# Output normalised on ScalarE and scaled on VectorE in whole-tile instructions, reciprocals on GpSimd: a cross-attention kernel on one core

## The chip, the cores and the metric

The kernel runs on one core of one Trainium2 chip. Times are device microseconds of one execution, and the time of a kernel is the median of its runs. The engines are named as in the profile: PE (TensorE) with PEld for its weight loads, DVE (VectorE), ACT (ScalarE), POOL (GpSimd) and SP, which here only issues DMAs.

## What is computed

For 64 batches, x is 256x512 and the context c is 256x384, all in float32:

```python
text_p  = x @ W_text + b_text            # 256x512
audio_p = c @ W_audio + b_audio          # 256x512
Q = layer_norm(text_p, g1, beta1)
K = layer_norm(audio_p, g2, beta2)
alpha = softmax(Q @ K.T / sqrt(512))
H = (alpha @ audio_p) @ W_out + b_out
out = layer_norm(H + x, g_out, beta_out)
```

`layer_norm` takes mean and variance over the last axis of 512, with 1e-5 added to the variance.

## The kernel before, in words

The batches go through a software pipeline written out by hand (`manual_schedule`): every engine runs its instructions in the order in which the code issues them. A batch's 256 rows are two tiles of 128 partitions, and most tensors are [128, 2, 512] or its transpose in four chunks.

One pass of the loop `for b in range(B - 2)` (L856) works on several batches at once:

- `at = Attention(b)`: scores of batch b into PSUM (`ps_sc`, L511), the negated row maxima on DVE (`maxima`, L521, tile `nmx`), the exponentials on ACT with their row sums in `den` (`exponentials`, L528), the reciprocals of the sums on DVE (`reciprocals`, L538, `rden`), the division of the exponentials on ACT (`divide_e`, L542), their store to DRAM and fetch in squares of 32 rows, from which DVE's 32x32 transposes make the transposed tile in the next pass (`turn_e`).
- q and then k of batch b + 2 (`Blocks`, L454 to L497): a product of 256 rows by 512 columns is made of seven half-size products in the manner of Strassen. `products` (L465) gives PE one or two of them for one PSUM bank; the pool `p_pj` has six banks, taken in turn. `leave` (L476, the adds of L483) evicts one product on DVE and adds it into the rows. The sums of inputs that the seven products need are formed by POOL (`sum_x`, L304 to L307, tile `xsum`; `sum_c`, L319 to L322, tile `csum`, or `zsum` for the output).
- After q and k, ACT squares the rows to get the variance (`square`, L380), POOL makes the reciprocal root by an add and a power of -0.5 (`rstd_of`, L335 to L344), ACT scales the rows (`normalise`, L408), SP stores them (`store`, L418). They are fetched in squares a pass later (`fetch`), transposed on DVE (`turn`, L91 and L439), and scaled and shifted per column on ACT (`affine`, L446, tiles `qT` and `kT`).
- `turn_next(b + 3)` (L728) transposes the inputs of batch b + 3 on DVE and forms their sums on POOL: `turn_x`, `sum_x`, `turn_c`, `sum_c`.
- `last` is the batch one pass older, b - 1: its context (`context`, L577), copied to `zT` by ACT (L584), the sums of that (`start_products`) and the seven output products (tile `ps_y`, rows `yr`), of which three are evicted at the head of the next pass.
- `done` is the batch two passes older, b - 2: after those evictions POOL adds x (`add_x`, L593), ACT takes sum and squares (`statistics`, L601 and L606, the negated mean `nm` and the sum of squares `ssq`), and DVE finishes the rows with two instructions for each of the two tiles: `shift` (L694), (y + nm) * g_out, and `settle` (L703), y * r + beta_out. SP stores the output (`store`, L713).

Head (batches 0 and 1) and tail (after the loop) are written out separately; in the tail `shift` and `settle` are used as well.

The order of one pass around the change is, as the code has it: scores, the last three evictions and add_x of `done`, `turn_e`, `turn_next`, maxima, exponentials, first q products and eviction, reciprocals, division, fetches and loads on SP, statistics of `done`, the other q products and evictions, squares of q, `q[b+1].turn`, the two shifts, context of `last`, affine of q, turn and affine of k, the two settles and the store of `done`, normalise and store of q, sums of zT, the whole of k, and then the output products of `last`.

Of the kernel before, what the change touches and what calls it, by code (L numbers as in the profile page):

```python
# [9 lines left out]
F32 = mybir.dt.float32  # L10
AF = mybir.ActivationFunctionType
ALU = mybir.AluOpType
# [3 lines left out]
P = 128  # L16
# [6 lines left out]
def kernel(  # L23
# [41 lines left out]
    nc = tc.nc  # L65
# [3 lines left out]
    H = w_text.shape[1]  # L69
    LT, ST = L // P, S // P  # L70
    DC, AC, HC = D // P, DA // P, H // P
    scale = 1.0 / math.sqrt(H)

    const = ctx.enter_context(tc.tile_pool(name="const", bufs=1))
# [4 lines left out]
    small = ctx.enter_context(tc.tile_pool(name="small", bufs=4))  # L79
# [26 lines left out]
    def load_squares(b):  # L106
        load_c(b)
        load_x(b)
# [23 lines left out]
    def row(v, name):  # L132
        t = const.tile([P, H], F32, tag=name, name=name)
        nc.sync.dma_start(t, v.rearrange("(o h) -> o h", o=1).broadcast_to([P, H]))
        return t
# [162 lines left out]
    def sum_x(xT):  # L298

        n = DC // 2  # L300
        part = lambda i, j: xT[:, j * n : (j + 1) * n, bass.ts(i, P)]
        s = work.tile([P, 4, n, P], F32, tag="xsum", name="xsum")
        add = nc.gpsimd.tensor_tensor
        add(s[:, 0], part(1, 0), part(1, 1), ALU.add)  # L304
        add(s[:, 1], s[:, 0], part(0, 0), ALU.subtract)  # L305
        add(s[:, 2], part(0, 0), part(1, 0), ALU.subtract)
        add(s[:, 3], part(0, 1), s[:, 1], ALU.subtract)  # L307
        ss = {
            1: part(0, 0), 2: part(0, 1), 4: part(1, 1),
            5: s[:, 0], 6: s[:, 1], 7: s[:, 2], 3: s[:, 3],  # L310
        }
        return {p: [ap[:, k, :] for k in range(n)] for p, ap in ss.items()}

    def sum_c(cT, tag="csum"):

        part = lambda i, j: cT[:, j, bass.ts(i, P)]
        s = work.tile([P, 5, P], F32, tag=tag, name=tag)
        add = nc.gpsimd.tensor_tensor
        add(s[:, 0], part(1, 0), part(1, 1), ALU.add)  # L319
        add(s[:, 1], s[:, 0], part(0, 0), ALU.subtract)  # L320
        add(s[:, 2:4], cT[:, 0:3:2, :P], cT[:, 0:3:2, P:], ALU.subtract)
        add(s[:, 4], part(0, 1), s[:, 1], ALU.subtract)  # L322
        return {
            1: [part(0, 0)], 2: [part(0, 1), part(0, 2)], 4: [part(1, 1), part(1, 2)],
            5: [s[:, 0], part(1, 2)], 6: [s[:, 1]], 7: [s[:, 2]], 3: [s[:, 4], s[:, 3]],
        }

    def weights_of_three(w_sb, name):
# [3 lines left out]
            ws[n].append(w_sb[:, 2, k2 * H2 : (k2 + 1) * H2])  # L332
        return ws

    def rstd_of(var, n, total=False):  # L335

        ve = small.tile([P, n], F32, tag="ve", name="ve")
        if total:
            nc.gpsimd.tensor_scalar(ve, var, 1.0 / D, EPS, ALU.mult, ALU.add)
        else:  # L340
            nc.gpsimd.tensor_scalar(ve, var, EPS, None, ALU.add)  # L341
        r = small.tile([P, n], F32, tag="rstd", name="rstd")
        nc.gpsimd.tensor_tensor(r, ve, nhalf[:, :n], ALU.pow)  # L343
        return [r[:, t : t + 1] for t in range(n)]  # L344

    class Projection:
# [57 lines left out]
        def normalise(self):  # L404
            for t in range(self.nt):
                row = self.rows[:, t, :]
                if self.centred:
                    nc.scalar.mul(row, row, self.r[t])  # L408
                else:
                    nc.scalar.activation(  # L410
                        row, row, AF.Identity, bias=self.nmr[:, t : t + 1], scale=self.r[t]
                    )
# [86 lines left out]
    class Attention:  # L499
# [36 lines left out]
        def reciprocals(self):  # L536
            self.rden = small.tile([P, LT], F32, tag="rden", name="rden")
            nc.vector.reciprocal(self.rden, self.den)  # L538

        def divide_e(self):  # L540
            for t in range(LT):
                nc.scalar.mul(self.e[:, t, :], self.e[:, t, :], self.rden[:, t : t + 1])  # L542
# [52 lines left out]
        def statistics(self):  # L595

            self.nm = small.tile([P, LT], F32, tag="nm", name="nm")
            self.ssq = small.tile([P, LT], F32, tag="ssq", name="ssq")
            for t in range(LT):
                junk = work.tile([P, D], F32, tag="junk", name="junk")  # L600
                nc.scalar.activation(  # L601
                    junk, self.y[:, t, :], AF.Identity, scale=-1.0 / D, accum_out=self.nm[:, t : t + 1]
                )
            for t in range(LT):
                junk = work.tile([P, D], F32, tag="junk", name="junk")
                nc.scalar.activation(  # L606
                    junk,
                    self.y[:, t, :],
                    AF.Square,
                    bias=self.nm[:, t : t + 1],  # L610
                    accum_out=self.ssq[:, t : t + 1],
                )
            self.r = dict(enumerate(rstd_of(self.ssq, LT, total=True)))

        def start_output(self):
            self.y = work.tile([P, LT, H], F32, tag="yr", name=f"y_{self.b}")
            self.mv = small.tile([P, LT, 2], F32, tag="mvy", name="mvy")
            self.ps_y = {}
# [99 lines left out]
    def turn_x(b):  # L718
        xT = work.tile([P, DC, L], F32, tag="xT", name=f"xT_{b}")
        turn(xT, blocks[b][1], DC)  # L720
        return xT

    def turn_c(b):
        cT = work.tile([P, AC, S], F32, tag="cT", name=f"cT_{b}")
        turn(cT, blocks[b][0], AC)
        return cT

    def turn_next(b):  # L728
        xT[b] = turn_x(b)
        xs[b] = sum_x(xT.pop(b))  # L730
        cT[b] = turn_c(b)
        cs[b] = sum_c(cT.pop(b))

    def add_bias(b):
        xb = rows[b][0]
# [4 lines left out]
    q, k, xT, cT, rows = {}, {}, {}, {}, {0: (x_0, c_0)}  # L740
# [31 lines left out]
    cs = {1: sum_c(cT[1])}  # L772
# [79 lines left out]
    go_sb = row(g_out, "go")  # L852
    beo_sb = row(beta_out, "beo")

    done = last = None
    for b in range(B - 2):  # L856
        three = b + 3 < B
        at = Attention(b)
        at.scores()
        if done:  # L860
            done.o.leave(3)
            done.o.leave(7)
            done.o.leave(4)
            done.add_x()
        if last:
            last.turn_e()
        if three and b:
            turn_next(b + 3)
        at.maxima()
        at.exponentials()  # L870
        q2 = q[b + 2] = Blocks("q", b + 2, xs.pop(b + 2), wt_blocks, bt_sb)
        q2.products(1, 2)
        q2.leave(1)
        at.reciprocals()
        at.divide_e()
        if b:
            q[b + 1].fetch()
            k[b + 1].fetch()
        at.store_e()
        if b + 4 < B:  # L880
            load_squares(b + 4)
        at.fetch_e()
        rows[b + 1] = load_rows(b + 1)
        if done:
            done.statistics()
        q2.products(6, 5)
        q2.leave(6)
        q2.leave(2)
        q2.leave(5)
        q2.products(7, 3)  # L890
        q2.leave(3)
        q2.leave(7)
        q2.products(4)
        q2.leave(4)
        q2.square()
        q2.scales()
        if three and not b:
            turn_next(b + 3)
        q[b + 1].turn()
        if done:  # L900
            done.shift(0)
            done.shift(1)
        if last:
            last.context()
        q[b + 1].affine(g1_sb, be1_sb)
        k[b + 1].turn()
        k[b + 1].affine(g2_sb, be2_sb)
        if done:
            done.settle(0)
            done.settle(1)  # L910
            done.store()
        q2.normalise()
        q2.store()
        if last:
            last.start_products()
        k2 = k[b + 2] = Blocks("k", b + 2, cs.pop(b + 2), wa_blocks, ba_sb)
        k2.products(1, 2)
        k2.leave(1)
        k2.products(6, 5)
        k2.leave(6)  # L920
        k2.leave(2)
        k2.leave(5)
        k2.products(7, 3)
        k2.leave(3)
        k2.leave(7)
        k2.products(4)
        k2.leave(4)
        k2.square()
        k2.scales()
        k2.normalise()  # L930
        k2.store()
        if last:
            last.o.products(1, 2)
            last.o.leave(1)
            last.o.products(6, 5)
            last.o.leave(6)
            last.o.leave(2)
            last.o.leave(5)
            last.o.products(7, 3)
            last.o.products(4)  # L940
        done, last = last, at


    at = Attention(B - 2)
# [112 lines left out]
```

## Time and profile before

| what | value |
|---|---|
| median of 3 runs | 1422.26 us (1420.84 to 1422.74) |
| the profiled execution | 1420.47 us, of which the span is 1418.70 us |
| mean granted TensorE clock | 0.998 |
| DMA | 322.61 MB, 227 GB/s over the span |
| ACT waits for nmx before the exponentials | 245.7 us in 64 waits |
| DVE waits for the exponentials before rden | 29.4 us in 60 waits |
| DVE waits for ps_q | 25.4 us in 107 waits |
| shift in the loop (L694) | 120 instructions, 726 ns each |
| settle (L703) | 124 instructions, 1065 ns each |

A row of the timeline gives the start in us from the start of the span, the duration from the first start to the last end of a group, the engine, the line, the operation, the tiles written and read, and the count; in brackets the idle time ahead of it and what ended it. A group of several instructions of one kind is one row, and consecutive instructions of an engine overlap by some tens of ns. Line numbers are those of the kernel before.

### The profile page before, as it was taken

The page shows a single profiled execution, that of the slowest core. Times are in us where ns is not written, and L with a number is a line of the kernel's source. Part 1 is how long each engine was busy: PE and PEld are TensorE (multiplying, and loading weights), DVE is VectorE, ACT ScalarE, POOL GpSimd, SP SyncE. Part 2 cuts the span into 40 slices and gives each one's busy share as a digit, 9 for nine tenths or more (in the row PEclk, how much of TensorE's full clock was granted, in tenths as well). Part 3 has the DMA queues.
Part 4 walks back from the last instruction along what each step waited for, and adds up shares of the span by engine and source line. Part 5 has one row for each costly group of instructions (what it writes and reads, how often), then busy time and mean ns, then how long its engine had stood idle before and what let it go on. Part 6 is the DMA issues. An engine that isn't in the chain of part 4 may idle for free.

```text
span 1418.7 us, 23330 instructions
## 1 busy us (share of the span) xinstructions
PE 1405.0 (99%) x6441; PEld 1220.9 (86%) x6441; DVE 1273.3 (90%) x2134; ACT 931.8 (66%) x2293; POOL 875.2 (62%) x1295
## 2 busy tenths in 40 slices
PE   9999999999999999999999999999999999999997
PEld 5788888888888888888888888888888888888885
DVE  5889999999999999999999999999999999999987
ACT  4666676676676676766766766766767667667662
POOL 5557556666666666566566665666665755666645
PEclk9999999999999999999999999999999999999999
DMA  8898887887888788788878887887887888788763
GB/s 207 228 246 229 242 244 209 242 240 216 237 233 234 228 230 238 233 226 236 244 217 236 239 224 228 238 229 229 229 238 232 225 239 242 216 238 241 205 200 109
DMA packets 450582, 322.61 MB, mean 227 GB/s; under 512 B 154900, under 2 KB 382996, under 8 KB 450452
## 3 DMA queue, kind: packets, MB, share of 16 engines
q1 hardware_dynamic: 450356, 320.98, 80.4%
q8 instruction: 53, 0.87, 0.3%
q14 instruction: 77, 0.63, 0.2%
q10 hardware_dynamic: 96, 0.13, 0.0%
HBM read 204.09 MB, written 116.92 MB: 226 GB/s over the span
## 4 chain that ended last, share of the span: by engine, by line
PE 94%; DMA 2%; DVE 1%; POOL 1%; SPq 1%; issue 1%; ACT 0%; POOLq 0%; DVEq 0%; ACTq 0%
PE ps_q L472 26%; PE ps_y L472 21%; PE ps_k L472 20%; PE ps_sc L511 15%; PE ps_z L577 11%; DMA qq<-qd 0%; DMA xq<-in_x_dram 0%; DMA qd<-qr 0%; DMA wt<-in_L_xattn_W_text_dram 0%; SPq L150 0%; DMA bt<-in_L_xattn_b_text_dram 0%; POOL rstd L343 0%; POOL ve L341 0%; DVE qr L483 0%; DVE st L267 0%
## 5 line engine op out<-in xcount | busy, mean ns | idle before, releaser
L341 POOL TENSOR_SCALAR ve<-var 128x2 f32<-128x2 f32 x126 | 43.6, 346 | 310.8 <-ACT junk L380 310.8
L511 PE MATMUL ps_sc<-kT,qT 128*128 128x256 f32 x1024 | 231.7, 379 | 1.9 <-ACT kT L446 1.9
L528 ACT ACTIVATE e<-ps_sc,nmx 128x256 f32<-128x256 f32 x128 | 59.5, 469 | 245.7 <-DVE nmx L521 245.7
L483 DVE TENSOR_TENSOR qr<-ps_q,qr 128x512 f32<-128x512 f32 x378 | 188.1, 511 | 35.8 <-PE ps_q L472 23.3
L511 PEld LDWEIGHTS ps_sc<-kT,qT 128*128 128x128 f32 x1024 | 194.2, 190 | 29.6 <-ACT kT L446 2.9
L483 DVE TENSOR_TENSOR kr<-ps_k,kr 128x512 f32<-128x512 f32 x378 | 188.2, 512 | 24.7 <-PE ps_y L472 0.5
L483 DVE TENSOR_TENSOR yr<-ps_y,yr 128x512 f32<-128x512 f32 x372 | 185.1, 511 | 24.1 <-DVE yr L483 0.9
L593 POOL TENSOR_TENSOR yr<-yr,x 128x512 f32<-128x512 f32 x124 | 157.0, 1274 | 58.0 <-DVE yr L483 58.0
L577 PE MATMUL ps_z<-eT,c 128*128 128x256 f32 x768 | 176.5, 379 | 0.1
L472 PE MATMUL ps_q<-wtsum,xsum 128*128 128x256 f32 x756 | 173.6, 379 | 0.0
L343 POOL TENSOR_TENSOR rstd<-ve,nhalf 128x2 f32<-128x2 f32 (+1 forms) x194 | 158.9, 819 | 16.1
L472 PE MATMUL ps_k<-wa,cT 128*128 128x256 f32 x630 | 166.8, 379 | 0.0
L472 PE MATMUL ps_y<-wao,zT 128*128 128x256 f32 x620 | 164.2, 379 | 0.0
L577 PEld LDWEIGHTS ps_z<-eT,c 128*128 128x128 f32 x768 | 145.8, 190 | 20.7 <-ACT e L528 0.5
L472 PEld LDWEIGHTS ps_q<-wtsum,xsum 128*128 128x128 f32 x756 | 143.6, 190 | 19.9 <-POOL xsum L305 0.5
L380 ACT ACTIVATE junk<-kr 128x512 f32<-128x512 f32 x126 | 79.3, 629 | 96.8 <-DVE kr L483 96.8
L446 ACT ACTIVATE qT<-qT,columns 128x256 f32<-128x256 f32 x256 | 132.8, 591 | 8.3 <-DVE qT L91 8.3
L472 PEld LDWEIGHTS ps_k<-wa,cT 128*128 128x128 f32 x630 | 119.6, 190 | 16.2
L446 ACT ACTIVATE kT<-kT,columns 128x256 f32<-128x256 f32 x256 | 132.2, 589 | 1.1 <-DVE kT L91 0.9
L472 PEld LDWEIGHTS ps_y<-wao,zT 128*128 128x128 f32 x620 | 117.7, 190 | 16.0
L408 ACT ACTIVATE kr<-kr,rstd 128x512 f32<-128x512 f32 x126 | 84.1, 714 | 69.9 <-POOL rstd L343 69.9
L703 DVE SCALAR_TENSOR_TENSOR yr<-yr,rstd,beo 128x512 f32<-128x512 f32 x124 | 127.4, 1065 | 0.6 <-POOL rstd L343 0.6
(150 smaller groups left out, 2946.4 us busy)
## 6 DMA issues: line engine op xcount, KB each, us to landing
kd<-kr SPq DMA_DIRECT2D x64, 512.0 KB, 3.1
kq<-kd SPq DMA_DIRECT2D x256, 128.0 KB, 3.4
qd<-qr SPq DMA_DIRECT2D x64, 512.0 KB, 5.1
qq<-qd SPq DMA_DIRECT2D x256, 128.0 KB, 3.3
xq<-in_x_dram SPq DMA_DIRECT2D x252, 128.0 KB, 2.9
x<-in_x_dram SPq DMA_DIRECT2D x63, 512.0 KB, 3.9
out_dram<-yr SPq DMA_DIRECT2D x62, 512.0 KB, 5.0
cq<-in_ctx_dram SPq DMA_DIRECT2D x252, 96.0 KB, 2.5
```

Of the source, the lines that this page charges most:

```text
L341: nc.gpsimd.tensor_scalar(ve, var, EPS, None, ALU.add)
L343: nc.gpsimd.tensor_tensor(r, ve, nhalf[:, :n], ALU.pow)
L380: nc.scalar.activation(junk, self.rows[:, t, :], AF.Square, scale=1.0 / math.sqrt(H), accum_out=self.var[:, t : t + 1],)
L408: nc.scalar.mul(row, row, self.r[t])
L446: nc.scalar.activation(self.T[:, k, :], self.T[:, k, :], AF.Identity, bias=bet[:, k : k + 1], scale=gam[:, k : k + 1],)
L472: nc.tensor.matmul(bank[:, j, :], lhsT=side, rhs=w, start=(i == 0), stop=(i == len(pairs) - 1))
L483: add = lambda o, i0, i1: nc.vector.tensor_tensor(o, i0, i1, ALU.add)
L511: nc.tensor.matmul(self.sc[:, t, :], lhsT=self.qT[:, k, bass.ts(t, P)], rhs=self.kT[:, k, :], start=(k == 0), stop=(k == HC - 1),)
L528: nc.scalar.activation(self.e[:, t, :], self.sc[:, t, :], AF.Exp, bias=self.nmx[:, t : t + 1], accum_out=self.den[:, t : t + 1],)
L577: nc.tensor.matmul(ps[:, j, :], lhsT=self.c_sb[:, s, bass.ts(lo + j, P)], rhs=self.eT[:, s, :], start=(s == 0), stop=(s == ST - 1),)
L593: nc.gpsimd.tensor_tensor(self.y[:, t, :], self.y[:, t, :], self.xb[:, t, :], ALU.add)
L703: nc.vector.scalar_tensor_tensor(self.y[:, t, :], self.y[:, t, :], self.r[t], beo_sb, ALU.mult, ALU.add)
```

## The change

- `reciprocals_aside` replaces `reciprocals` in the loop: POOL raises `den` to the power -1, with a constant tile `mone` set once. It is issued right after the exponentials, ahead of the first q products.
- `sum_c` of batch b + 3 is taken out of `turn_next` and issued behind that power, so on POOL it comes after it.
- `statistics` gets two small POOL products: `nmr` = `nm` * r, one for each tile.
- `normalise` of the output: ACT computes y * r + nmr for each of the two tiles. It is issued after `context` and ahead of the affine of q, where the shifts stood before the context.
- `scale_and_shift`: DVE multiplies both tiles at once by g_out and then adds beta_out, 128x1024 each, with the vectors repeated over the two tiles by a broadcast access pattern. It stands where the settles stood.

Head, tail and the loop's PE instructions are the same, but for the memset of `mone`.

```diff
--- before.py
+++ after.py
@@ -332,6 +332,9 @@
             ws[n].append(w_sb[:, 2, k2 * H2 : (k2 + 1) * H2])
         return ws
 
+    mone = const.tile([P, 2], F32, tag="mone", name="mone")
+    nc.gpsimd.memset(mone, -1.0)
+
     def rstd_of(var, n, total=False):
 
         ve = small.tile([P, n], F32, tag="ve", name="ve")
@@ -537,6 +540,10 @@
             self.rden = small.tile([P, LT], F32, tag="rden", name="rden")
             nc.vector.reciprocal(self.rden, self.den)
 
+        def reciprocals_aside(self):
+            self.rden = small.tile([P, LT], F32, tag="rden", name="rden")
+            nc.gpsimd.tensor_tensor(self.rden, self.den, mone, ALU.pow)
+
         def divide_e(self):
             for t in range(LT):
                 nc.scalar.mul(self.e[:, t, :], self.e[:, t, :], self.rden[:, t : t + 1])
@@ -611,6 +618,24 @@
                     accum_out=self.ssq[:, t : t + 1],
                 )
             self.r = dict(enumerate(rstd_of(self.ssq, LT, total=True)))
+            self.nmr = small.tile([P, LT], F32, tag="nmry", name="nmr")
+            for t in range(LT):
+                nc.gpsimd.tensor_tensor(
+                    self.nmr[:, t : t + 1], self.nm[:, t : t + 1], self.r[t], ALU.mult
+                )
+
+        def normalise(self):
+            for t in range(LT):
+                row = self.y[:, t, :]
+                nc.scalar.activation(
+                    row, row, AF.Identity, bias=self.nmr[:, t : t + 1], scale=self.r[t]
+                )
+
+        def scale_and_shift(self):
+
+            for v, op in ((go_sb, ALU.mult), (beo_sb, ALU.add)):
+                v = v.rearrange("p (o h) -> p o h", o=1).broadcast_to([P, LT, H])
+                nc.vector.tensor_tensor(self.y, self.y, v, op)
 
         def start_output(self):
             self.y = work.tile([P, LT, H], F32, tag="yr", name=f"y_{self.b}")
@@ -729,7 +754,6 @@
         xT[b] = turn_x(b)
         xs[b] = sum_x(xT.pop(b))
         cT[b] = turn_c(b)
-        cs[b] = sum_c(cT.pop(b))
 
     def add_bias(b):
         xb = rows[b][0]
@@ -868,10 +892,12 @@
             turn_next(b + 3)
         at.maxima()
         at.exponentials()
+        at.reciprocals_aside()
+        if three and b:
+            cs[b + 3] = sum_c(cT.pop(b + 3))
         q2 = q[b + 2] = Blocks("q", b + 2, xs.pop(b + 2), wt_blocks, bt_sb)
         q2.products(1, 2)
         q2.leave(1)
-        at.reciprocals()
         at.divide_e()
         if b:
             q[b + 1].fetch()
@@ -896,18 +922,17 @@
         q2.scales()
         if three and not b:
             turn_next(b + 3)
+            cs[b + 3] = sum_c(cT.pop(b + 3))
         q[b + 1].turn()
-        if done:
-            done.shift(0)
-            done.shift(1)
         if last:
             last.context()
+        if done:
+            done.normalise()
         q[b + 1].affine(g1_sb, be1_sb)
         k[b + 1].turn()
         k[b + 1].affine(g2_sb, be2_sb)
         if done:
-            done.settle(0)
-            done.settle(1)
+            done.scale_and_shift()
             done.store()
         q2.normalise()
         q2.store()
```

## The prediction

> **What bounds the kernel now.** I read the busy times first, then the chain of work that ended last, then two stretches as long as one pass of the batch loop, and then the timeline of one pass, engine by engine. The page:
>
> ```profile
> PE 1405.0 (99%) x6441; PEld 1220.9 (86%) x6441; DVE 1273.3 (90%) x2134; ACT 931.8 (66%) x2293; POOL 875.2 (62%) x1295
> ...
> PE 94%; DMA 2%; DVE 1%; POOL 1%; SPq 1%; issue 1%; ACT 0%; POOLq 0%; DVEq 0%; ACTq 0%
> ```
>
> TensorE (PE) is busy all the time and is the chain. The stretches (length, then busy time of PE, PEld, DVE, ACT, POOL, the granted clock, DMA share, GB/s):
>
> ```profile
> 693.00:714.58 21.58, 21.58 (x102) 19.00 (x101) 19.76 (x34) 14.57 (x36) 13.62 (x21) 1.00 0.81 230
> 714.58:736.17 21.58, 21.58 (x102) 19.00 (x101) 19.75 (x34) 14.57 (x36) 13.64 (x21) 1.00 0.82 233
> ```
>
> Every pass takes 21.58 us: 100 matmuls (q 28, scores 16, context 12, k 22, output 22), 0.2158 us apart, without a gap. So time taken off VectorE (DVE) wins nothing in the loop by itself; the question is whether the change makes PE wait. DVE's time is nearly spoken for (19.76 of 21.58), and its order is fixed, so I follow one pass. DVE, ACT and POOL from the timeline (start, duration):
>
> ```profile
> 714.30 0.65 DVE L521 TENSOR_REDUCE nmx<-ps_sc 128x2 f32<-128x512 f32 x1
> 714.99 0.47 ACT L528 ACTIVATE e<-ps_sc,nmx 128x256 f32<-128x256 f32 x1 [3.96 <-DVE nmx L521]
> 715.84 0.73 POOL L307 TENSOR_TENSOR xsum<-xT,xsum 128x256 f32<-128x256 f32 x1
> 716.04 0.17 DVE L538 RECIPROCAL rden<-den 128x2 f32<-128x2 f32 x1 [0.49 <-ACT e L528]
> 716.24 0.91 ACT L542 ACTIVATE e<-e,rden 128x256 f32<-128x256 f32 x2 [0.23 <-DVE rden L538]
> 716.52 0.47 POOL L319 TENSOR_TENSOR csum<-cT 128x128 f32<-128x128 f32 x1
> 720.85 1.37 DVE L694 SCALAR_TENSOR_TENSOR yr<-yr,nm,go 128x512 f32<-128x512 f32 x2
> 720.91 1.01 ACT L584 COPY zT<-ps_z 128x512 f32<-128x512 f32 x2
> 721.82 2.08 ACT L446 ACTIVATE qT<-qT,columns 128x256 f32<-128x256 f32 x4
> 723.36 2.06 DVE L703 SCALAR_TENSOR_TENSOR yr<-yr,rstd,beo 128x512 f32<-128x512 f32 x2
> 723.70 1.18 POOL L321 TENSOR_TENSOR zsum<-zT 128x256 f32<-128x256 f32 x1
> 725.35 0.68 DVE L483 TENSOR_TENSOR kr<-ps_k,ba 128x512 f32<-128x512 f32 x1
> 730.54 0.71 POOL L343 TENSOR_TENSOR rstd<-ve,nhalf 128x2 f32<-128x2 f32 x1
> 731.28 1.33 ACT L408 ACTIVATE kr<-kr,rstd 128x512 f32<-128x512 f32 x2 [1.13 <-POOL rstd L343]
> 735.88 0.65 DVE L521 TENSOR_REDUCE nmx<-ps_sc 128x2 f32<-128x512 f32 x1
> ```
>
> The reader is to see a ring. The maxima (714.30) release the exponentials on ACT; ACT then divides, takes the statistics and squares, and copies zT without a pause (716.24 to 721.82). DVE goes from its first k eviction (725.35) to the next maxima (735.88) without a listed wait: 10.53 us. Today nothing of ACT's second half holds DVE, since the shifts and settles need only statistics that POOL has early.
>
> PE is held when a PSUM bank is late. The pool has six banks, taken in turn, and a pass takes twelve: four each for q, k and output. The output's pair (7, 3), the eleventh, takes the bank of the fifth, k's pair (1, 2), which is free when DVE has evicted k's products 1 and 2:
>
> ```profile
> 728.68 0.59 PE L472 MATMUL ps_y<-waosum,zsum 128*128 128x256 f32 x2
> ...
> 726.86 0.75 DVE L483 TENSOR_TENSOR kr<-ps_k,kr 128x256 f32<-128x256 f32 x2
> ```
>
> Product 2 is the first of these two evictions and ends near 726.86 + 0.42 = 727.28; the products start at 728.68. So a first delay of 1.40 us on DVE is free, and all beyond it stops PE.
>
> **The change, step by step,** in the frame of that pass.
>
> *Reciprocal to POOL.* DVE loses 0.17 us, and its 0.49 us wait. The power takes 0.71 us (the row of 730.54, 128x2 with the same operation) and 0.03 to ACT (731.25 to 731.28). POOL is in the xsum until 716.52, so ACT divides at 716.52 + 0.74 = 717.26 instead of 716.24: **+1.02 us**. Behind it on POOL the four csum sums move by 0.73, to an end near 719.3; PE wants the first at 722.64. POOL's 1.24 us wait for the output's squares covers the rest. Bounds: 0.71 to 1.07 us, the row at 721.72, which ran while DVE worked on two SBUF tensors.
>
> *ACT up to the normalisation.* Divide to zT is 720.91 - 716.24 = 4.67 us of unbroken work, so zT starts at 721.93. Its two copies take 0.74 (0.47, and 0.27 to the next start) as PE's context is done by then. The new pair of normalisations starts at 722.67. POOL's root is there: the squares' sum comes 1.02 later, root at 721.87, two small products of 0.26 each by the nearest row (L395, 264 ns, 128x1) at 722.4; if each cost 0.46 like the 128x128 sum L320, 0.15 late. The pair's own price has a row in the head, the same form with two per-partition operands:
>
> ```profile
> 23.97 1.52 ACT L410 ACTIVATE kr<-kr,nmr,rstd 128x512 f32<-128x512 f32 x2 [0.51 <-POOL nmr L395]
> ...
> 1399.60 1.42 DVE L703 SCALAR_TENSOR_TENSOR yr<-yr,rstd,beo 128x512 f32<-128x512 f32 x2 [0.60 <-POOL rstd L343]
> ```
>
> 722.67 + 1.52 + 0.04 hand-off = **724.23**, when DVE may begin to scale. Today's settle began at 723.36, and DVE, rid of 1.29 us of shifts, stands idle for some 2 us.
>
> *Two whole-tile instructions.* No row has a 128x1024 tensor-tensor on SBUF. Evictions take 0.69 us at 512 and 0.42 at 256, that is 0.15 + 1.05 ns an element, so 1.22 us at 1024; the sums of two halves by a broadcast operand cost no more than the others. Two, with 0.10 between dependent ones and 0.07 overlap after: 2.47 us. Beside them POOL runs zsum. Today's settles take 2.06 us there and 1.42 in the tail row above: 0.64 lost, and POOL's L321 takes 1148 ns against 735 for the same shape in csum. The new pair reads two SBUF tensors too and meets the same sums, so I add 0.64: **3.11 us**. Bounds: 2.47 (no collision), and 2.47 x 2.06/1.42 = 3.6 (in proportion).
>
> The Trainium skill (SBUF — State Buffer, "Who interferes with whom") says that such an instruction and a GpSimd one that reads SBUF exclude each other for a whole instruction. By it the second scaling waits out one 735 ns sum, less the 0.10 gap: 3.10 us as an estimate, and 3.56 if the sum before also gets in first; L703's spread of 732 to 1841 ns agrees with whole blocks rather than a slope.
>
> *The ring's sum.* Maxima to scaling 724.23 - 714.30 = 9.93; scaling 3.11; first k eviction to next maxima 10.53. That is **23.57 us against 21.58: +1.99 a pass.** POOL, ACT's later work and the queues have room in it: affines end at 728.0, PE's scores start after 731; q's store on SP goes from 727.11 to 729.4, and with the 5.1 us of landing it is there at 734.5, before q's fetch at 735.1; k's store and both fetches move with the k evictions, so only as far as the ring does. The output's store keeps its place ahead of q's.
>
> *Passes.* b = 2 to 60 have an output to finish: 59 x 1.99 = 117.4. In the last pass there is no xT and cT to turn (2.14 us less on DVE), so the ring is slack and gives about 0.4 back. PE enters the tail with the 1.40 us margin used up, less the tail's own wait for maxima: about 1 off. Head and tail code is unchanged but for one memset. The profiled execution took 1420.47 us (span 1418.70): 1420.5 + 116 = **1536.5 us**; the median of the runs lies 1.8 above that execution, so I give 1537.
>
> **Rivals.**
> (1) No collision with POOL: +1.35 a pass, 59 x 1.35 - 1 = 79, **1500 us**. For: zsum might end before the scaling. Against: its last two sums start after 724.3 by the same count.
> (2) Heavier: power 1.07 (+0.36), scaling 3.6 (+0.5), small products late (+0.15): +3.0 a pass, **1596 us**. For: L703's longest, 1841 ns. A lower PE clock belongs here: PE would idle 2 us a pass; it would count only below 21.58/23.57 = 0.92 of the clock. The page's clock is 0.998 and falls (0.70) only in the last 8 us, with PE idle throughout.
> The Trainium skill (TensorE: Matmul & The Clock Gate, "Part 1: The HAM clock gate") has the clock halve after an idle window of some 3.4 us. By that, 2 us would leave 1537 standing and 3 us be near the edge; no run here shows it.
> (3) Not slower: DVE's 10.53 us are paced by PE rather than filled with work. If 2.0 of them are slack, the evictions close up, the bank comes in time, and PE stays at 21.58: **1420 us**. For: DVE does wait for PE at the q evictions. Against: the rows themselves fill it, 2 x (3 x 0.69 + 4 x 0.42) = 7.5 plus 0.70 + 1.20 + 0.94 of transposes = 10.3.
> (4) The scaling pair runs at two elements a cycle as L184's copies do (426 ns for 512): 1.5 us, +0.38 a pass, 59 x 0.38 - 1 = 21, **1441 us**. Against: it reads two tensors.
> Faster by more than 0.2% would need head or tail to shrink by 3 us, and their code is untouched.
>
> **How the numbers follow.** Forecast (1515 to 1565) 0.58; rival 1 0.14; rival 2 0.15; rival 3 0.07; rival 4 0.03; faster 0.03. The range takes in the forecast and rivals 1 and 2 as far as 1590 and leaves out rivals 3, 4, faster and the top of rival 2, under 0.2: 1490 to 1590. Slower by over 0.2% (about what a measurement here can tell from no change): 0.58 + 0.14 + 0.15 + 0.03 = 0.90; within it 0.07; faster 0.03.
>
> **What would show it.** Right: passes of 23.0 to 24.2 us; PE idle before ps_y<-waosum,zsum, released by DVE's kr eviction; DVE idle before the first scaling, released by ACT's normalisation; scaling pair near 3.1 us; the divide released by POOL's power, 2.3 us after the first exponential's start (now 716.24 - 714.99 = 1.25). Wrong: PE still without gaps (rival 3), or DVE's wait released by something other than ACT, or evictions that stretch. The weakest number is the scaling pair beside POOL: 0.1 us in it is 6 us in the whole.

## The result, and the profile after

The changed kernel takes 1524.67 us (1524.50 to 1525.07, four runs) against 1421.55 us (1420.57 to 1422.74) for the kernel before: 1.0726 times, interval 1.0713 to 1.0739. The forecast was 1537 us in 1490 to 1590. Its profiled execution took 1524.76 us with a span of 1522.9, that is 104.2 us more span than before. Line numbers from here on are those of the changed kernel, a few higher than before.

The page's busy times and its chain:

```profile
PE 1419.7 (93%) x6441; PEld 1215.8 (80%) x6441; DVE 1239.5 (81%) x1952; ACT 1010.9 (66%) x2413; POOL 965.4 (63%) x1478
...
DVE 39%; ACT 16%; POOL 13%; PE 12%; issue 10%; DMA 5%; SPq 4%; DVEq 1%; POOLq 0%
```

No engine is now busy all the time. DVE has less to do than before and yet leads the chain, followed by ACT and POOL, as when engines wait for each other in turn. Two passes as stretches (columns as before), from one row maxima to the next:

```profile
696.97:720.24 23.27, 21.82 (x101) 18.92 (x101) 19.13 (x32) 15.89 (x38) 15.05 (x24) 1.00 0.85 214
720.24:743.51 23.27, 21.82 (x101) 18.91 (x101) 19.12 (x31) 15.88 (x38) 15.06 (x24) 1.00 0.81 213
```

A pass takes 23.27 us instead of 21.58. PE is now idle for 1.45 us of it. The timeline of the second one, with the rows of the ring in order:

```profile
720.24 0.65 DVE L524 TENSOR_REDUCE nmx<-ps_sc 128x2 f32<-128x512 f32 x1
722.47 0.71 POOL L545 TENSOR_TENSOR rden<-den,mone 128x2 f32<-128x2 f32 x1
723.21 0.91 ACT L549 ACTIVATE e<-e,rden 128x256 f32<-128x256 f32 x2 [1.26 <-POOL rden L545]
727.89 0.82 ACT L591 COPY zT<-ps_z 128x512 f32<-128x512 f32 x2
728.61 1.52 ACT L630 ACTIVATE yr<-yr,nmr,rstd 128x512 f32<-128x512 f32 x2
730.16 1.23 DVE L638 TENSOR_TENSOR yr<-yr,go 128x1024 f32<-128x1024 f32 x1 [2.97 <-ACT yr L630]
730.24 1.74 POOL L321 TENSOR_TENSOR zsum<-zT 128x256 f32<-128x256 f32 x1
731.43 1.63 DVE L638 TENSOR_TENSOR yr<-yr,beo 128x1024 f32<-128x1024 f32 x1
731.94 1.44 POOL L322 TENSOR_TENSOR zsum<-zT,zsum 128x128 f32<-128x128 f32 x1
732.98 0.68 DVE L486 TENSOR_TENSOR kr<-ps_k,ba 128x512 f32<-128x512 f32 x1
735.06 0.67 PE L475 MATMUL ps_y<-waosum,zsum 128*128 128x256 f32 x2 [1.45 <-DVE kr L486]
```

Read it from bracket to bracket. ACT waits 1.26 us for POOL's reciprocals. DVE waits 2.97 us for ACT's normalisation, with the k evictions queued behind. PE waits 1.45 us for DVE's k eviction, which frees the bank of its output products, just where the prediction put it. From the first k eviction (732.98) to the next maxima (743.51) DVE works on without a wait, 10.53 us as before.

The waits of the whole run (us in total, times, longest) say the same:

```profile
DVE yr L638 <- ACT yr L630: 166.5, 60, 3.0
PEld ps_y L475 <- issue: 111.1, 60, 2.2
...
PE ps_y L475 <- DVE kr L486: 88.8, 60, 1.8
ACT e L549 <- POOL rden L545: 82.0, 62, 5.9
```

DVE and PE have sixty waits each, one for each pass with an output to finish (b = 2 to 61); ACT has 62, one for every pass. The 111.1 us of PE's weight loader, put down to "issue", are 60 stops ahead of the same products: in the pass above the loader resumes at 735.03, after 1.83 us, and PE at 735.06. They and PE's 88.8 us overlap and are not to be added.

### The profile page after: what moved, and what is told of

Read it like the earlier page. It is cut to its first block, busy times and chain, and to the rows that moved or that the text cites. A ratio compares the mean times of both kernels' runs of the same rounds, so it can differ in the third digit from the quotient of the medians.

```text
span 1522.9 us, 23331 instructions
## 1 busy us (share of the span) xinstructions
PE 1419.7 (93%) x6441; PEld 1215.8 (80%) x6441; DVE 1239.5 (81%) x1952; ACT 1010.9 (66%) x2413; POOL 965.4 (63%) x1478
## 4 chain that ended last, share of the span: by engine, by line
DVE 39%; ACT 16%; POOL 13%; PE 12%; issue 10%; DMA 5%; SPq 4%; DVEq 1%; POOLq 0%
DVE yr L486 12%; DVE yr L638 11%; DVE kr L486 9%; PE ps_y L475 7%; ACT yr L630 6%; DVE xT L91 5%; DMA cq<-in_ctx_dram 4%; ACT e L549 4%; SPq L88 3%; POOL xsum L304 3%; POOL xsum L305 3%; POOL rden L545 3%; POOL xsum L306 3%; ACT junk L608 2%; ACT zT L591 2%
## 5 line engine op out<-in xcount | busy, mean ns | idle before, releaser
L344 POOL TENSOR_SCALAR ve<-var 128x2 f32<-128x2 f32 x126 | 27.5, 218 | 298.9 <-ACT junk L383 293.8
L638 DVE TENSOR_TENSOR yr<-yr,go 128x1024 f32<-128x1024 f32 x60 | 73.8, 1229 | 166.5 <-ACT yr L630 166.5
L475 PE MATMUL ps_y<-waosum,zsum 128*128 128x256 f32 x372 | 105.1, 391 | 89.3 <-DVE kr L486 88.8
L475 PEld LDWEIGHTS ps_y<-waosum,zsum 128*128 128x128 f32 x372 | 65.6, 189 | 118.5 <-issue 111.1
L346 POOL TENSOR_TENSOR rstd<-ve,nhalf 128x2 f32<-128x2 f32 (+1 forms) x194 | 137.5, 709 | 16.2
```

The lines of the kernel that those rows point to most:

```text
L475: nc.tensor.matmul(bank[:, j, :], lhsT=side, rhs=w, start=(i == 0), stop=(i == len(pairs) - 1))
L638: nc.vector.tensor_tensor(self.y, self.y, v, op)
```

## The experiments

**Theory**: a ring sets the pass: maxima (DVE), exponentials (ACT), reciprocals (POOL), ACT's work up to the normalisation, scaling, k and output evictions and transposes (DVE), next maxima. What lengthens the ring lengthens the pass, as long as it is above PE's 21.58 us. **Rivals**: the load itself is the price (more work on ACT and POOL, collisions of DVE and POOL), or one of the two moved operations costs its time wherever it stands. Each edit below is against the changed kernel; ratios are to the kernel before. All of them compute the whole reference.

**1. The reciprocals alone** (`recip_only`): output finished by shift and settle as before, with the two `nmr` products gone.

```diff
         q[b + 1].turn()
+        if done:
+            done.shift(0)
+            done.shift(1)
         if last:
             last.context()
-        if done:
-            done.normalise()
...
         if done:
-            done.scale_and_shift()
+            done.settle(0)
+            done.settle(1)
             done.store()
```

> The reciprocals on GpSimd and the moved csum as in the change; the output keeps the shifts and settles of before. Ring theory: the divide comes some 1.0 us later, but nothing of ACT's second half holds VectorE, so the pass stays at PE's 21.58 us: 1420 to 1425 us, 2 us of it from the head. Rival (the move of the reciprocals costs its 1.02 us by itself): 60 x 1.02 more, 1482 us.

1422.72 us, 1.0003 (0.9994 to 1.0012); passes of 21.58 us. The page of this kernel:

```profile
PE 1405.2 (99%) x6441; PEld 1220.5 (86%) x6441; DVE 1241.1 (87%) x2072; ACT 926.2 (65%) x2293; POOL 899.1 (63%) x1358
```

DVE is busy 32 us less than in the kernel before (1273.3), by the reciprocals and by settles that collide less with POOL's later sums (842 ns each on average instead of 1065), and nothing comes of it: PE is the bound. And the division's 1.0 us delay costs nothing where DVE does not wait for ACT's second half.

**2. The reciprocals back on DVE** (`recip_back`), the normalisation kept on ACT.

```diff
         at.exponentials()
-        at.reciprocals_aside()
...
         q2.leave(1)
+        at.reciprocals()
         at.divide_e()
```

> The change with the reciprocals back on VectorE. Ring theory: the divide follows the maxima by 1.94 instead of 2.97 us, the pass goes from 23.27 to 22.24 us, and the head's 2 us go: 1524.7 - 58 x 1.03 - 2 = 1463 us. Rival (the ACT work and the collision with GpSimd set the time, the reciprocals are hidden): 1520 to 1525 us.

1461.5 us, 1.0277 (1.0262 to 1.0293). Three rows of one pass:

```profile
735.51 0.65 DVE L524 TENSOR_REDUCE nmx<-ps_sc 128x2 f32<-128x512 f32 x1
737.45 0.91 ACT L549 ACTIVATE e<-e,rden 128x256 f32<-128x256 f32 x2 [0.23 <-DVE rden L541]
744.41 1.23 DVE L638 TENSOR_TENSOR yr<-yr,go 128x1024 f32<-128x1024 f32 x1 [1.45 <-ACT yr L630]
```

The division comes 1.94 us behind the maxima and not 2.97, the scaling 8.90 and not 9.92, and the pass takes 22.26 us. So the same move of the reciprocals that is free in experiment 1 costs 63 us in the presence of the normalisation (1524.7 against 1461.5). So the rival of a fixed price falls for it, and its load on POOL, the same in experiment 1, is not the price either.

**3. The scaling behind the k evictions** (`scale_late`). Every instruction of the change is kept; only the place of two of DVE's and of the store differs.

```diff
         k[b + 1].affine(g2_sb, be2_sb)
-        if done:
-            done.scale_and_shift()
-            done.store()
...
         k2.leave(4)
+        if done:
+            done.scale_and_shift()
+            done.store()
         k2.square()
```

> The change with the two whole-tile scalings and the output's store moved behind the k evictions on VectorE, nothing else. Ring theory: the wait for ACT no longer stands before the k evictions, the bank comes in time, VectorE's work fits into 21.58 us, and PE is the bound again: 1420 to 1426 us; GpSimd is idle there, so the scaling pair takes 2.4 to 2.5 us instead of 2.82. Rival (the added ACT and GpSimd work is what costs): above 1490 us.

1422.72 us, 1.0007 (0.9998 to 1.0016), passes of 21.58 us: all of the loss is gone, although ACT, POOL and DVE have the same instructions. The page of this kernel, and rows of one pass:

```profile
PE 1405.8 (99%) x6441; PEld 1220.7 (86%) x6441; DVE 1214.5 (85%) x1952; ACT 998.1 (70%) x2413; POOL 845.5 (60%) x1478
...
726.66 0.46 POOL L322 TENSOR_TENSOR zsum<-zT,zsum 128x128 f32<-128x128 f32 x1
...
728.60 1.22 DVE L638 TENSOR_TENSOR yr<-yr,go 128x1024 f32<-128x1024 f32 x1
729.85 1.23 DVE L638 TENSOR_TENSOR yr<-yr,beo 128x1024 f32<-128x1024 f32 x1
730.99 0.68 DVE L486 TENSOR_TENSOR yr<-ps_y,bao 128x512 f32<-128x512 f32 x1
```

The scaling finds its input ready and POOL done with zsum, and takes 2.39 us (728.60 to 730.99) against 2.82. The load is not the price; the place in DVE's queue is. It is also not faster than the kernel before: DVE busy falls from 1273.3 to 1214.5 us, and PE's 100 matmuls a pass stay.

**4. Scaling by tile** (`per_tile`): multiply tile 0, tile 1, add tile 0, tile 1.

```diff
-                v = v.rearrange("p (o h) -> p o h", o=1).broadcast_to([P, LT, H])
-                nc.vector.tensor_tensor(self.y, self.y, v, op)
+                for t in range(LT):
+                    nc.vector.tensor_tensor(self.y[:, t, :], self.y[:, t, :], v, op)
```

> The change with the scaling in four instructions of one tile each: multiply tile 0 and 1, then add tile 0 and 1. Ring theory: the first starts when ACT has normalised tile 0, 0.7 us sooner, the four take as long as the two but for 0.1: the pass falls by some 0.5 us to 22.8: about 1493 us; up to 1525 if the shorter instructions meet GpSimd's sums more often. Rival (the whole-tile form saves 0.15 us of fixed cost per instruction): 1542 us.

1529.73 us, 1.0756 (1.0741 to 1.0771): a miss, 5 us slower than the whole-tile form and not 30 us faster, and above even the 1525 us that was allowed for more collisions. The timeline shows that the start was right and the duration wrong:

```profile
732.43 1.70 DVE L638 TENSOR_TENSOR yr<-yr,go 128x512 f32<-128x512 f32 x2 [2.25 <-ACT yr L630]
732.79 0.79 POOL L320 TENSOR_TENSOR zsum<-zsum,zT 128x128 f32<-128x128 f32 x1
733.54 1.17 POOL L321 TENSOR_TENSOR zsum<-zT 128x256 f32<-128x256 f32 x1
734.05 2.08 DVE L638 TENSOR_TENSOR yr<-yr,beo 128x512 f32<-128x512 f32 x2
734.68 0.90 POOL L322 TENSOR_TENSOR zsum<-zT,zsum 128x128 f32<-128x128 f32 x1
```

The view of line 638 gives the shortest, the median and the longest of the additions in ns, over the whole run:

```profile
L638 DVE TENSOR_TENSOR yr<-yr,beo x120: 679/943/1218, 102.2 to 1481.3; 128x512 f32<-128x512 f32 x120
```

The first multiplication starts 9.21 us after the maxima (723.22), 0.71 earlier, as counted. But the four take 3.62 us up to the k eviction at 736.05. Uncollided they would take an estimated 2.4 (four of the shortest, 0.68 us, each overlapping the next by 0.08), no more than the two long ones of experiment 3. So fixed cost is not the reason, as the rival had it. POOL's three sums are stretched beside them as well, to 0.79, 1.17 and 0.90 us from 0.46, 0.74 and 0.46 in experiment 3. The rows read as DVE and POOL taking turns, with one more sum let in at each change of DVE's instruction; no run moved the sums away to test that in this form.

**5 and 6. The same 0.7 us on POOL, on the ring and off it** (`dose_on`, `dose_off`). A second power into a tile that nobody reads, ahead of the reciprocals, or behind the csum sums.

```diff
+            first = small.tile([P, LT], F32, tag="first", name="first")
+            nc.gpsimd.tensor_tensor(first, self.den, mone, ALU.pow)
             nc.gpsimd.tensor_tensor(self.rden, self.den, mone, ALU.pow)
```

```diff
             cs[b + 3] = sum_c(cT.pop(b + 3))
+        again = small.tile([P, LT], F32, tag="first", name="first")
+        nc.gpsimd.tensor_tensor(again, at.den, mone, ALU.pow)
```

> The change with the power of the reciprocals done twice on GpSimd, the first time into a tile that nobody reads; the same instruction, just ahead of the real one. Ring theory: all of it adds to the pass, 0.66 to 0.71 us: 1524.7 + 59 x 0.68 = 1565 us. Rival (PE or a throughput is the bound and GpSimd has room): 1525 us.

> The change with the same second power, into a tile that nobody reads, but behind the csum sums, where GpSimd waits 1.6 us for ACT. Ring theory: it lies off the ring, 1524 to 1528 us. Rival (GpSimd's load or its collisions set the time): 1565 us as in the other.

On the ring 1564.68 us, 1.1013 (1.0994 to 1.1031), passes of 23.94; off it 1525.3 us, 1.0734 (1.0718 to 1.0750), passes of 23.28. One row of each kernel's page:

```profile
PE 1437.7 (92%) x6441; PEld 1229.1 (79%) x6441; DVE 1240.4 (79%) x1952; ACT 1010.6 (65%) x2413; POOL 1007.8 (64%) x1540
```

```profile
PE 1420.4 (93%) x6441; PEld 1216.4 (80%) x6441; DVE 1240.3 (81%) x1952; ACT 1011.2 (66%) x2413; POOL 1006.6 (66%) x1540
```

POOL is as busy in one as in the other, to 1.2 us, and the times lie 39 us apart, 0.66 us in each of 59 passes. That settles ring against load.

No version beat the kernel before; the two that equal it (1 and 3) stand on PE's 21.58 us a pass.

## Why the prediction was right, step by step

The mechanism, the engine that waits, and the place where PE stops were right. Its own terms, with the measured ones beside them (a steady pass):

| term of the ring | predicted us | measured us |
|---|---|---|
| maxima to division, with POOL's power | 2.96 | 2.97 |
| maxima to zT | 7.63 | 7.65 |
| maxima to the normalisation | 8.37 | 8.37 |
| maxima to the scaling | 9.93 | 9.92 |
| scaling pair, to the first k eviction | 3.11 | 2.82 |
| first k eviction to the next maxima | 10.53 | 10.53 |
| pass | 23.57 | 23.27 |

The one mis-sized term is the scaling pair beside POOL. I gave it the whole 0.64 us that the settles lose there. The multiplication in fact runs free (1.23 us) and the addition loses 0.40 (1.63 against 1.23 in experiment 3). The base of 2.47 was good: 2.39 measured without collision. So of the 0.29 us too many, 0.21 are the collision and 0.08 the base; with the other terms the pass was 0.30 too long, over 58 passes 17 us.

Adding up: 58 passes (b = 2 to 59) at +1.69 make 98.0. The measured 104.2 us of span has 6.2 more, from three places that the sum had as gains or not at all:
- The first passes: 2.1 us. For b = 0 the power stands on POOL behind the sums of the preparation, eight for batch 2's inputs and four for the output weights; ACT waits 5.9 us once, and in the next pass DVE waits 3.4 us for the fetched exponentials. I had followed POOL's queue in the steady pass only.
- Some 2.6 us, most of it in six passes of 23.5 to 23.6 us, the rest in the first of the 58, which were quicker than 21.58 before (21.2 us for b = 2 and 3). In four of the six one DVE eviction starts 0.46 us behind the last instead of 0.10, in the last of them the last k eviction; why is open, and it wasn't tried.
- 1.5 us from b = 60 to the end, where I had hoped for 0.6.

So the span's sum missed by 11.8 us and not by 58 x 0.30 = 17.4: these three places hold 5.6 us more than the sum gave them. That part of its nearness is luck.

The smaller steps: the two small products take 0.19 us each, not 0.26, and hide as said. DVE stands idle for 2.97 us before the scaling and not for "some 2": its waits for PE's q products, 25.4 us in the whole run before, shrank to 4.1 as well, which I had not taken off. That wait is no term of the sum. The queues had room, with 12 waits of DVE for the fetched k squares (6.7 us in all), most of them inside its wait for ACT. Rival 1 (no collision) came nearest among the rivals; the measured time lies between it and the forecast. The clock of rival 2 stayed out: 0.999 in the changed kernel. Rival 3 (DVE's 10.53 us hold slack) fell: the figure is the same to 0.01 us in both kernels. Rival 4 fell too: the pair takes 2.39 us even without collision, not 1.5.

The rule of the Trainium skill (SBUF — State Buffer, "Who interferes with whom") made the collision 0.63 us as an estimate; the measured loss is 0.40. It has right that both sides lose: L321 and L322 stretch, to 1.74 and 1.44 us, each over one scaling, and the addition is late as well. But DVE's addition loses less than the sum's 735 ns; why is not shown.

## What to carry to other kernels

Here, freeing an engine that was busy 90% of the time gained nothing while another was busy without a gap; ask first which wait would move. Before moving work between engines that run in order, write down who is queued behind the instruction that would now wait, and add up the ring that closes from one pass to the next: if it stays under the bound's pass, the move is free (experiment 1), and if not, every 0.1 us in it is paid in every pass (experiment 5). A loss of this kind can be mended by the place of the waiting instruction alone, with no operation changed (experiment 3).

## What the runs showed of the hardware that was not expected

- A DVE instruction with two SBUF inputs and a POOL sum of SBUF tensors stretch each other, and how much depends on how they interleave and not on the amount of work alone: the same 2x1024 elements lost 0.43 us in two instructions and an estimated 1.2 us in four. Fewer, longer instructions lost less on DVE, and more on POOL (the sum of L321 for `zsum` 1694 ns on average in the changed kernel, 1159 in experiment 4, 730 in experiment 3).
- PE's stop of 1.45 us a pass left its granted clock at 0.999. In `dose_on`, with a stop of some 2.1 us in most passes, the mean was 0.986, and 0.96 from 800 to 1000 us; the passes did not lengthen there, since the ring and not PE set them.
- What lowered that clock can be read in the same trace. After the first passes and up to the tail it was half of full in ten stretches of 3.41 us, the first at 611.7 and the last at 1041.8 us, 47.8 us or about two passes apart, and full otherwise. On a grid of 3.41 us counted from the first, PE was busy 29 to 41% of the stretch just before each of the ten, and 43% or more of every other stretch from 90 to 1490 us. The prediction took 2 us of idle time as safe; here a stop of 2.1 us cost clock where it fell almost whole into one such stretch, and none where it was split over two. `per_tile` has one stretch of half clock, at 552.3 us, behind one that was 44% busy, so the edge is known only roughly; the ends of matmuls are modelled in these traces.
